# Graph attention on one core: node products and ACT's copies moved to the head of a step, products with Wv of the last units moved behind the last row products, sums and adds of the last units on POOL

## The chip, the cores and the metric

The kernel runs on one core of a Trainium2 chip. The metric is the device time of one execution in microseconds (us). The kernel before takes 2296.72 us, the median of 5 runs (2286.04 to 2301.53).

## What is computed

There are N = 12500 nodes with 128 features, and E = 212500 edges, sorted by their destination. An edge has 128 features and a weight. There are 8 heads of 16 features. Cut to what matters:

```
h = max(layernorm(x), 0)
q, v = h @ Wq.T + bq, h @ Wv.T + bv
k = edge_attr @ Wk.T + bk
in_m, out_m, diag_m = q[src].k, q[dst].k, q[src].q[dst]   # per edge and head
score = (softmax over dst of each of the three, summed) * weight ** lam
h = segment_sum(score * v[dst], dst)
out = x + leaky_relu(h @ Wo.T + bo, 0.1)
```

Since `v[dst]` is the same for all edges of a node, a node's h is v times a sum of scores. So the edges give each node three numerators and three denominators per head, and the nodes are finished from these sums.

## The kernel before

**Preparation.** The nodes are normalised and multiplied by Wq; q is written to a table in DRAM (`q_table`), and once more as three bf16 terms.

**The main loop over edges.** The edges are cut into 416 blocks of 512, and these into S = 5 streams, each of which runs through its own part of the edges. One pass of the loop, a *step*, takes a block of one stream: step number g is stream s = g % 5 of *turn* t = g // 5. There are 84 turns and 420 steps, and 10 more passes of the loop with no edges of their own. In a step:

- POOL issues four indirect DMAs (L656), each of which gathers 128 rows of q for a later block (`gather(g + 9)`), into one of 11 buffers `qq`.
- SP fetches edge features for block g + 6.
- PE makes k of block g + 1 (`project`, L1115 and L1117), spreads the q of the destinations by one-hot matrices (`spread_q`, L1126, "row products" below; ACT copies them to `qq`, L1128), and transposes the features of block g + 2 (`turn`, L1107; ACT copies them, L1109).
- DVE multiplies and reduces block g (`logits`, L1137, L1138, L1140). L1137 reads the gathered rows and the row products.
- ACT makes one-hots of block g + 3 (L1101, L1102).
- Once in a turn, for all five streams at a time and a turn or two later, come the softmax sums. At s = 0 PE transposes the logits (`l_ps`, L1153, `far_ps`, L1162) and the sums of the turn before (`b_ps`, L1226). At s = 1 DVE scans for the maximum (L1170, L1173). At s = 2 ACT makes the powers (`up`, `down`, `keep`, L1183 to L1188) and PE the sums by row (`w_ps`, L1239, copied by ACT, L1244). At s = 3 DVE multiplies (L1194) and makes two scans (L1198). At s = 4 PE shows where nodes end (`d_ps`, L1214), ACT makes `sel` of it (L1217, L1218), and SP writes the sums by row to DRAM (L1251).

**The nodes.** A *unit* is 256 nodes. Two units make an object of the class `Nodes`. Twenty pairs are finished within the loop, each over four turns from an even turn t on, when its sums are complete; they begin in turns 18, 22, 26, 30, 32 and so on, the last in turn 82:

- turn t: load sums and x (s = 0); normalise (ACT, s = 2 and 3); scores (six short DVE instructions on 96 or 32 columns, L1034 to L1039, s = 2)
- turn t + 1: transpose h (`turn`, L1043, copied by ACT, L1046, s = 1); the product with Wv (`project_v`: L1049 and L1051 on PE) and its weighing by the scores (DVE, L1059), s = 4
- turn t + 2: transpose (s = 1); the product with Wo (`project_o`: L1049 and L1051 on PE), 0.1 times it (ACT, L1069), the maximum (DVE, L1070) and the sum with x (DVE, L1071), s = 4
- turn t + 3: store (SP, s = 0)

All this stands in `nodes_between`, which is called near the end of a step. So PE's product at s = 4 comes behind the step's row products, transposes and d_ps, and DVE's part comes behind the step's L1140.

**The last units.** Nine units, in five objects `rest` (the last has one unit), have sums that are complete only at the end, and for some of them in two parts. `begin_rest` loads and normalises their x, transposes it and makes the products with Wv in the last steps. Its argument `at` is g - 411; LOOK is 9, so `at` = 9 is the first of the ten passes without edges. The products stay in PSUM buffers that the main loop no longer needs. After the loop the sums are loaded, the two parts added (DVE, L1032), the scores made and weighed, and the same transposes, products and adds follow, one object behind the other.

**What sets the order.** Every instruction goes through `pin`, which ties it behind the instruction pinned before it on its engine. So the order on each engine is the order in which the Python code runs, and an engine that waits holds up all that is pinned behind. Small results in PSUM (l_ps, far_ps, att_ps, keep, w_ps, d_ps, b_ps and all node_ps) share three buffers:

```python
        def small(shape, name):
            return ps.tile(shape, F32, name=name, tag="small", bufs=3)
```

The row products qd_ps have one buffer, so PE can make the next ones only when DVE's L1137 has read it.

Of the kernel before, what the change touches and what calls it, by code (L numbers as in the profile page):

```python
# [10 lines left out]
AF = mybir.ActivationFunctionType  # L11
# [9 lines left out]
SLOPE = 0.1  # L21
# [451 lines left out]
def ordered_path(ctx: ExitStack, tc: tile.TileContext, flag, x, src, dst, edge_attr, edge_weight,  # L473
# [19 lines left out]
    nc = tc.nc  # L493
    N, F = x.shape
    E = src.shape[0]
    P = 128
    NI = -(-N // P)
    NP = P * NI
    BE, JN = 512, 4
    NB = -(-E // BE)  # L500
    S = 5
    T = (NB + S - 1) // S
# [18 lines left out]
    def parts_of(u):  # L521

        return [s for s in range(S)
                if (s == 0 or START * s + RATE - NEAR < UN * (u + 1))
                and (s == S - 1 or UN * u < START * (s + 1) + RATE + NEAR)]

    def stored_at(u):

        of = parts_of(u)
        t = -(-(UN * (u + 1) + NEAR - START * of[0]) // RATE)  # L530
        return t + 2 if len(of) == 1 and t < T else None
# [57 lines left out]
    LOOK, QQ, AHEAD, EA = 9, 11, 6, 7  # L589
# [6 lines left out]
    def pin(inst):  # L596

        engine = str(inst.ins.engine)
        if engine in pinned:
            tc.add_manual_dep(inst.ins, pinned[engine], mybir.DependencyInfo(  # L600
                mybir.DependencyClass.NoSync, mybir.DependencyReason.DATA), reason="in order")
        pinned[engine] = inst.ins.name
        return inst
# [48 lines left out]
    def gather(g):  # L652
        if g < S * T:
            qq = gath.tile([P, JN, 2, F], F32, name="qq")
            for j in range(JN):
                rows = pin(nc.gpsimd.indirect_dma_start(  # L656
                    out=qq[:, j, 0, :], out_offset=None, in_=q_table,
                    in_offset=bass.IndirectOffsetOnAxis(
                        ap=src_i[:, g % S * G + g // S, j:j + 1], axis=0)))
                if (g - LOOK, j) in behind:  # L660
                    tc.add_manual_dep(rows.ins, behind[g - LOOK, j], mybir.DependencyInfo(
                        mybir.DependencyClass.Sync, mybir.DependencyReason.SCHED_ONLY),
                        reason="close behind the products")
            qqs[g] = qq
# [15 lines left out]
    with tc.tile_pool(name="prep", bufs=1) as prep, \  # L680
# [22 lines left out]
        for s in range(S):  # L703
            at = s * G * BE
            pin(nc.sync.dma_start(bases[:, :, s:s + 1], dst[None, at:at + G * BE + 1:BE, None]))
            n = min(T, (E - at) // BE)
# [287 lines left out]
    class Nodes:  # L994
# [26 lines left out]
        def normalize(self, lo, hi):  # L1021
            if lo == 0 and self.h is None:
                self.h = fin.tile([P, JN, F], F32, name="h", bufs=4)
            for b in range(lo, min(hi, self.n)):
                n = 2 * self.of[b // 2] + b % 2
                pin(nc.scalar.activation(self.h[:, b, :], self.x[:, b, :], AF.Relu,
                                         bias=shift[:, n:n + 1], scale=inv[:, n:n + 1]))

        def scores(self):
            n = self.n  # L1030
            for ab, more in self.more:
                pin(nc.vector.tensor_add(ab, ab, more))  # L1032
            den, num = self.ab[:, :n, 0:H3], self.ab[:, :n, H3:]
            pin(nc.vector.tensor_scalar(den, den, 1e-30, None, op0=ALU.max))  # L1034
            pin(nc.vector.reciprocal(den, den))
            pin(nc.vector.tensor_mul(num, num, den))
            score = self.score = fin.tile([P, JN, HEADS], F32, name="score")
            pin(nc.vector.tensor_add(score[:, :n], num[:, :, 0:HEADS], num[:, :, HEADS:2 * HEADS]))
            pin(nc.vector.tensor_add(score[:, :n], score[:, :n], num[:, :, 2 * HEADS:]))  # L1039
# [12 lines left out]
                                     stop=(b == self.n - 1)))  # L1052

        def project_v(self, to):
            self.product(to, bv3, wv)
            self.weigh(to)

        def weigh(self, to):
            pin(nc.vector.tensor_mul(  # L1059
# [5 lines left out]
        def project_o(self, to):  # L1065
            n = self.n
            self.product(to, bo3, wo)
            o, y = self.h[:, :n], self.x[:, :n]
            pin(nc.scalar.activation(o, to[:, :n], AF.Copy, scale=SLOPE))  # L1069
            pin(nc.vector.tensor_max(o, o, to[:, :n]))  # L1070
            pin(nc.vector.tensor_add(y, o, y))  # L1071

        def store(self):
            for i, u in enumerate(self.of):
# [8 lines left out]
    pairs, todo = {}, sorted((stored_at(u), u) for u in range(NU) if stored_at(u) is not None)  # L1083
# [3 lines left out]
    rest = [u for _, u in todo] + [u for u in range(NU) if stored_at(u) is None]  # L1087
    rest = [Nodes(rest[i:i + 2]) for i in range(0, len(rest), 2)]

    with tc.tile_pool(name="work", bufs=2) as work, \  # L1090
# [56 lines left out]
        def small(shape, name):  # L1147
            return ps.tile(shape, F32, name=name, tag="small", bufs=3)
# [106 lines left out]
        def later(f, t):  # L1255
            if 0 <= t < T:
                f(t)

        def nodes_between(t, s):
            new, old = pairs.get(t - t % 2), pairs.get(t - t % 2 - 2)  # L1260
            even = t % 2 == 0
            if new and even and s == 0:
                new.load_sums()
                new.load_x()
            if new and even and s == 2:
                new.normalize(0, 2)
                new.scores()
            if new and even and s == 3:
                new.normalize(2, 4)
            if new and not even and s == 1:  # L1270
                new.turn(small([P, JN, P], "node_ps"))
            if new and not even and s == 4:
                new.project_v(small([P, JN, F], "node_ps"))
            if old and even and s == 1:
                old.turn(small([P, JN, P], "node_ps"))
            if old and even and s == 4:
                old.project_o(small([P, JN, F], "node_ps"))
            if old and not even and s == 0:
                old.store()

# [6 lines left out]
        def spare():  # L1287
            return gath.tile([P, JN, 2, F], F32, name="qq").rearrange("p j i f -> p (j i f)")

        def halves():  # L1290
            return spare().rearrange("p (i j f) -> i p j f", i=2, j=JN)

        def begin_rest(at):
            if at in turned:
                late.update(zip(turned[at], halves()))
            if at in (LOOK - 1, LOOK):
                late[at - LOOK] = spare()
            for r, (of, begin) in enumerate(zip(rest, starts)):
                if at == begin:
                    to, of.h = halves()  # L1300
                    of.load_x(to)
                if at == begin + 2:
                    of.normalize(0, 4)
                if at == begin + 3:
                    of.hT = late[r]
                    of.turn(small([P, JN, P], "node_ps"))
                if at == LOOK + r:
                    of.held = ps.tile([P, JN, F], F32, name=holds[r], bufs=2 if r < 4 else 1)
                    of.product(of.held, bv3, wv)

# [10 lines left out]
        one_hots(2)  # L1321
        for g in range(end + 2 * S):
            s, t = g % S, g // S
            if g < end:
                gather(g + LOOK)
                fetch_edges(g + AHEAD)
            if g + 1 < end:
                project(g + 1)
                behind[g + 1, 0] = pinned[products]
                spread_q(g + 1)  # L1330
            if g + 2 < end:
                turn(g + 2)
            if g < end:
                logits(g)
            one_hots(g + 3)
            if s == 0:
                later(turn_logits, t - 1)
                later(turn_sums, t - 2)
            elif s == 1:
                later(scan_max, t - 1)  # L1340
            elif s == 2:
                later(powers, t - 1)
                later(to_rows, t - 2)
            elif s == 3:
                later(select, t - 1)
                later(scan_sums, t - 1)
                fetch(t + 2)
                fetch_rows(t + 2)
            else:
                later(show_ends, t - 1)  # L1350
                later(put_rows, t - 2)
            behind[g + 1, 2] = pinned[products]
            nodes_between(t, s)
            begin_rest(g - (end - LOOK))
            if g < S:
                of = [u for u in range(NU) if g in parts_of(u)]
                pin(nc.scalar.dma_start(
                    units(sums[g], of[0], len(of), 2 * H3),
                    blank[:, None, :].to_broadcast([P, len(of), 2 * 2 * H3])))


        for r, of in enumerate(rest):
            of.load_sums(*[late[k][:, r * JN * 2 * H3:(r + 1) * JN * 2 * H3].rearrange(
                "p (j c) -> p j c", j=JN) for k in (-1, 0)])
        for r in range(len(rest) + 2):
            if r < len(rest):
                rest[r].scores()
                rest[r].weigh(rest[r].held)
            if 0 <= r - 1 < len(rest):
                rest[r - 1].turn(small([P, JN, P], "node_ps"))  # L1370
            if 0 <= r - 2:
                rest[r - 2].project_o(small([P, JN, F], "node_ps"))
                rest[r - 2].store()


# [43 lines left out]
```

## Time and profile before

| what | us |
|---|---|
| median of 5 runs (lowest, highest) | 2296.72 (2286.04, 2301.53) |
| the profiled execution's own time | 2303.96 |
| its span, first to last instruction | 2302.2 |
| first L1137 on DVE, at | 144.15 |
| last L1137 on DVE, at | 2242.94 |
| first and last gather issued by POOL, at | 96.23, 2217.01 |
| granted TensorE clock, mean | 0.805 |

| engine | busy us | share |
|---|---|---|
| DVE | 2072.5 | 90% |
| PE | 1823.9 | 79% |
| ACT | 1650.1 | 72% |
| POOL | 1646.8 | 72% |

The lines of the profile that are quoted below have one of three forms. A group of instructions reads: line, engine, operation, out<-in, shapes, how often | busy us in all, mean ns of one | idle time before them, and what ended it. A wait reads: who <- whom: us in all, times, the longest. A line of the timeline reads: start, us, engine, line, operation, out<-in, how often, and in brackets the idle time of the engine before it and what ended that. "issue" stands for idle time in which the engine waited for nothing that the profile shows.

### The profile page before, as it was taken

Reading aid. Unit: us, or ns where it says so; the run is one execution under the profiler, and the core shown is the slowest. Engines: PE = TensorE matmul, PEld = TensorE weight load, DVE = VectorE, ACT = ScalarE, POOL = GpSimd, SP = SyncE. Lnnn points to the kernel's source line nnn. Section 1 sums busy time; section 2 is a strip of 40 time slices with the busy share of each in tenths; the row PEclk is TensorE's granted clock in tenths of the full one; section 3 lists DMA queues with packets and bytes.
Section 4 is the critical chain, followed back from the end, with each engine's and each line's share of the span. In section 5 each row is a group of like instructions: output and inputs, shape, how many; then the busy total and the mean of one; then the engine's idle time right before and its main releaser. Section 6 shows DMA issues by size and latency. Waiting matters only on the chain.

```text
span 2302.2 us, 36583 instructions
## 1 busy us (share of the span) xinstructions
PE 1823.9 (79%) x10781; PEld 1399.6 (61%) x10781; DVE 2072.5 (90%) x2180; ACT 1650.1 (72%) x3049; POOL 1646.8 (72%) x1716
## 2 busy tenths in 40 slices
PE   5538787878888888888888887888888878888885
PEld 4426565656666666666666666656666666666664
DVE  6779999989999999889999999998989899988984
ACT  5667777767777777677776777777777677776772
POOL 3577777777777777777777777777777777777740
PEclk8768889877877887779787788777777788877877
DMA  7785555555455555455554555555555555554531
GB/s 194 224 270 156 157 140 155 142 148 142 136 147 142 151 146 161 135 144 144 158 144 138 150 154 145 141 155 137 142 145 149 149 145 143 159 145 134 154 78 41
DMA packets 308902, 341.93 MB, mean 149 GB/s; under 512 B 139781, under 2 KB 227610, under 8 KB 308383
## 3 DMA queue, kind: packets, MB, share of 16 engines
q1 hardware_dynamic: 246259, 223.55, 32.6%
q0 software_dynamic: 54448, 112.96, 19.7%
q10 hardware_dynamic: 7984, 3.00, 0.5%
q8 instruction: 86, 1.41, 0.3%
q14 instruction: 125, 1.02, 0.1%
HBM read 308.22 MB, written 31.07 MB: 147 GB/s over the span
## 4 chain that ended last, share of the span: by engine, by line
PE 33%; ACT 22%; DVE 16%; DMA 13%; issue 12%; POOL 3%; SPq 1%; DVEq 0%; ACTq 0%; POOLq 0%
PE k_ps L1117 11%; DMA qq<-q_table,src_i 9%; PE eT_ps L1107 5%; ACT eT L1109 4%; PE qd_ps L1126 4%; DVE prod L1137 4%; ACT relb L1101 4%; DVE sum L1198 4%; ACT oh L1102 4%; DVE prod L1138 3%; ACT l L1160 3%; ACT qq L1128 3%; PE b_ps L1226 3%; POOL qq L656 3%; PE k_ps L1115 2%
## 5 line engine op out<-in xcount | busy, mean ns | idle before, releaser
L656 POOL DMA_INDIRECT qq<-q_table,src_i x1680 | 1609.9, 958 | 523.0 <-issue 318.5
L1140 DVE TENSOR_REDUCE lT<-prod 128x96 f32<-128x1536 f32 x420 | 736.3, 1753 | 14.3
L1117 PE MATMUL k_ps<-wk,eT 128*128 128x128 f32 x3360 | 603.4, 334 | 107.7 <-ACT eT L1109 65.8
L1117 PEld LDWEIGHTS k_ps<-wk,eT 128*128 128x128 f32 x3360 | 510.0, 232 | 253.3 <-ACT eT L1109 149.6
L1128 ACT COPY qq<-qd_ps 128x512 f32<-128x512 f32 x420 | 244.6, 582 | 456.3 <-PE qd_ps L1126 384.5
L1138 DVE TENSOR_TENSOR prod<-qq,k_ps 128x1024 f32<-128x1024 f32 x420 | 510.0, 1214 | 0.0
L1126 PE MATMUL qd_ps<-win,oh 126*128 126x128 bf16 x1680 | 199.6, 253 | 182.3 <-DVE prod L1137 166.3
L1137 DVE TENSOR_TENSOR prod<-qq,qd_ps 128x512 f32<-128x512 f32 x420 | 284.3, 677 | 65.4 <-ACT qq L1128 49.2
L1107 PE MATMUL eT_ps<-ident,ea 128*128 128x128 f32 x1680 | 326.2, 329 | 5.6 <-DVE found L955 5.6
L1101 ACT ACTIVATE relb<-relb,before 126x512 bf16<-126x512 bf16 x420 | 306.6, 730 | 0.0
L1126 PEld LDWEIGHTS <-oh 126*128 126x128 bf16 x1680 | 156.7, 115 | 217.2 <-issue 185.1
L1102 ACT ACTIVATE oh<-relb 126x512 bf16<-126x512 bf16 x420 | 264.6, 630 | 17.6 <-DMA qq<-q_table,src_i 4.3
L1109 ACT COPY eT<-eT_ps 128x512 f32<-128x512 f32 x420 | 247.3, 589 | 38.3 <-PE eT_ps L1107 36.3
L1107 PEld LDWEIGHTS eT_ps<-ident,ea 128*128 128x128 f32 x1680 | 230.9, 174 | 5.9 <-DVE found L955 5.9
L1226 PE MATMUL b_ps<-ident,sum 120*128 120x120 f32 x672 | 136.6, 333 | 112.8 <-ACT l L1160 112.8
L1226 PEld LDWEIGHTS b_ps<-ident,sum 120*128 120x128 f32 x672 | 99.1, 213 | 153.4 <-ACT l L1160 130.2
L1239 PE MATMUL w_ps<-back,sel 128*126 128x144 f32 x1344 | 190.9, 296 | 0.6 <-ACT back L1227 0.6
L1115 PE MATMUL k_ps<-b,ones 3*128 3x512 bf16 x420 | 185.7, 442 | 3.8 <-DVE prod L1138 3.4
L1239 PEld LDWEIGHTS w_ps<-back,sel 128*126 128x126 f32 x1344 | 172.7, 191 | 22.9 <-issue 18.7
L1227 ACT COPY back<-b_ps 128x480 f32<-128x480 f32 x168 | 97.5, 581 | 44.1 <-PE b_ps L1226 44.1
L1170 DVE TENSOR_TENSOR_SCAN u<-l,u,far_ps 120x512 f32<-120x512 f32 x83 | 105.5, 1271 | 1.8 <-ACT l L1160 1.8
L1198 DVE TENSOR_TENSOR_SCAN sum<-keep,sum,up 120x512 f32<-120x512 f32 x83 | 106.0, 1277 | 0.0
(187 smaller groups left out, 1857.8 us busy)
## 6 DMA issues: line engine op xcount, KB each, us to landing
ea<-in_edge_attr_dram SPq DMA_DIRECT2D x419, 256.0 KB
relb<-rel_d SPq DMA_DIRECT2D x84, 630.0 KB
qq<-q_table,src_i POOLq DMA_INDIRECT x1680
win<-q_table SPq DMA_DIRECT2D x420, 31.5 KB
q_table<-q SPq DMA_DIRECT2D x24, 384.0 KB
fa<-fa_d SPq DMA_DIRECT2D x420, 4.0 KB
sums<-rows SPq DMA_DIRECT2D x416, 7.9 KB
q_table<-xq SPq DMA_DIRECT2D x24, 256.0 KB
```

Source lines behind the costliest of these rows:

```text
L656: rows = pin(nc.gpsimd.indirect_dma_start(out=qq[:, j, 0, :], out_offset=None, in_=q_table, in_offset=bass.IndirectOffsetOnAxis(ap=src_i[: ...
L1101: pin(nc.scalar.activation(d, d, AF.Abs, bias=before[:K3]))
L1102: pin(nc.scalar.activation(oh, d, AF.Relu, bias=1.0, scale=-1.0))
L1107: pin(nc.tensor.transpose(eT_ps[:, j, :], eas[g][:, j * F:(j + 1) * F], ident))
L1109: pin(nc.scalar.copy(eT, eT_ps))
L1117: pin(nc.tensor.matmul(k_ps[:, j, :], eTs[g][:, j, :], wk, start=False, stop=(j == JN - 1)))
L1126: pin(nc.tensor.matmul(qd_ps[:, j, :], ohs[g][:, j * P:(j + 1) * P], d["win"][:, s, :], start=(j == 0), stop=(j == JN - 1)))
L1128: pin(nc.scalar.copy(qqs[g][:, :, 1, :], qd_ps))
L1137: pin(nc.vector.tensor_mul(prod[:, :, 2, :], qqs[g][:, :, 0, :], qds[g]))
L1138: pin(nc.vector.tensor_mul(prod[:, :, 0:2, :], qqs[g], ks[g][:, :, None, :].to_broadcast([P, JN, 2, F])))
L1140: pin(nc.vector.tensor_reduce(lTs[t][:, :, s, :], prod.rearrange("p j i (h d) -> p j (i h) d", d=DIM), AX.X, ALU.add))
L1239: pin(nc.tensor.matmul(w_ps[:, i].rearrange("p s c -> p (s c)"), d["sel"][:, j, lo:lo + 3, :].rearrange("p s w -> p (s w)"), d["back"][:, ...
```

## The change

1. A new function `nodes_before` is called at the head of each step. It makes the products of a pair at s = 4 (with Wv in odd turns, with Wo in even ones) and, with Wo, ACT's copy. They stood at the end of the same step. DVE's part (`weigh`; `add_x`, the maximum and the sum with x) stays at the end of the step.
2. The second transpose of the pair that ends after the loop's last turn (t = 84) is made at s = 2 in place of s = 1.
3. For the last units, the products with Wv move from `at` = 9, 10, 11, 12, 13 to `at` = 12, 13, 16, 16, 16, and the transpose of the fifth object from `at` = 9 to 12. In the steps 425 to 429 the last b_ps comes at `at` = 14 and the last w_ps at `at` = 16, ahead of the products there.
4. For the last units, POOL makes the sums of the two parts (`add_sums`, all objects one after the other, ahead of the first scores) and the sum with x. For the pairs in the loop there are no two parts to add, and DVE makes the sum with x as before.

```diff
+        def add_sums(self):
+            for ab, more in self.more:
+                pin(nc.gpsimd.tensor_add(ab, ab, more))
+
         def scores(self):
             n = self.n
-            for ab, more in self.more:
-                pin(nc.vector.tensor_add(ab, ab, more))
...
         def project_v(self, to):
+            self.held = to
             self.product(to, bv3, wv)
-            self.weigh(to)
...
         def project_o(self, to):
             n = self.n
             self.product(to, bo3, wo)
+            o = self.h[:, :n]
+            self.held = to
+            pin(nc.scalar.activation(o, to[:, :n], AF.Copy, scale=SLOPE))
+
+        def add_x(self, engine):
+            n, to = self.n, self.held
             o, y = self.h[:, :n], self.x[:, :n]
-            pin(nc.scalar.activation(o, to[:, :n], AF.Copy, scale=SLOPE))
             pin(nc.vector.tensor_max(o, o, to[:, :n]))
-            pin(nc.vector.tensor_add(y, o, y))
+            pin(engine.tensor_add(y, o, y))
...
+        def nodes_before(t, s):
+
+            new, old = pairs.get(t - t % 2), pairs.get(t - t % 2 - 2)
+            if new and t % 2 == 1 and s == 4:
+                new.project_v(small([P, JN, F], "node_ps"))
+            if old and t % 2 == 0 and s == 4:
+                old.project_o(small([P, JN, F], "node_ps"))
...
             if new and even and s == 2:
                 new.normalize(0, 2)
+                new.add_sums()
                 new.scores()
...
             if new and not even and s == 4:
-                new.project_v(small([P, JN, F], "node_ps"))
-            if old and even and s == 1:
+                new.weigh(new.held)
+            if old and even and s == (1 if t < T else 2):
                 old.turn(small([P, JN, P], "node_ps"))
             if old and even and s == 4:
-                old.project_o(small([P, JN, F], "node_ps"))
+                old.add_x(nc.vector)
...
-                if at == begin + 3:
+                if at == (begin + 3 if r < 4 else LOOK + 3):
                     of.hT = late[r]
                     of.turn(small([P, JN, P], "node_ps"))
-                if at == LOOK + r:
+                if at == LOOK + (3, 4, 7, 7, 7)[r]:
...
             s, t = g % S, g // S
+            nodes_before(t, s)
...
+        for of in rest:
+            of.add_sums()
         for r in range(len(rest) + 2):
...
                 rest[r - 2].project_o(small([P, JN, F], "node_ps"))
+                rest[r - 2].add_x(nc.gpsimd)
                 rest[r - 2].store()
```

## The prediction

> **What bounds the kernel now.** I read the busy shares first, then the waits, then the timeline turn by turn. On the page DVE looks like the bound, and the table of waits shows the idle time this change is aimed at:
>
> ```profile
> PE 1823.9 (79%) x10781; PEld 1399.6 (61%) x10781; DVE 2072.5 (90%) x2180; ACT 1650.1 (72%) x3049; POOL 1646.8 (72%) x1716
> ...
> L656 POOL DMA_INDIRECT qq<-q_table,src_i x1680 | 1609.9, 958 | 523.0 <-issue 318.5
> ```
>
> ```profile
> DVE h L1070 <- ACT h L1069: 52.3, 20, 4.1
> ...
> DVE h L1059 <- PE node_ps L1051: 28.5, 19, 1.9
> ```
>
> DVE stands still 80.8 us in 39 places, 76.6 us of it in 38 places of turns 18 to 82 of the main loop (the DVE waits of 200 to 2240 us: 48.1 + 28.5). One place, in the timeline of PE and DVE:
>
> ```profile
> 2057.74 0.59 PE L1126 MATMUL qd_ps<-win,oh 126*128 126x128 bf16 x4 [2.89 <-DVE prod L1137]
> ...
> 2059.78 0.63 PE L1049 MATMUL node_ps<-b,ones 3*128 3x512 bf16 x1
> 2060.34 2.08 PE L1051 MATMUL node_ps<-wo,hT 128*128 128x128 f32 x8
> ...
> 2063.35 0.69 DVE L1070 TENSOR_TENSOR h<-h,node_ps 128x512 f32<-128x512 f32 x1 [2.74 <-ACT h L1069]
> ```
>
> PE idles 2.89 us just before step 4's row products, makes the node product after them, and DVE then waits for it.
>
> But look at POOL. Its row reads 72%, yet there are 1680 gathers of 0.94 us with 0.30 us between them, whatever releaser is named: one starts each 1.25 us, without a break, from 96 to 2217 us. Twenty gathers are a turn: 25.0 us, with a few long ones 25.16. How far is DVE behind them? I compare the last gather of a step with the product (L1137) that reads it, at step 0 of turn 14 (first two rows) and of turn 83 (last two), in the timeline; the row between is step 3 of turn 15:
>
> ```profile
> 461.39 0.94 POOL L656 DMA_INDIRECT qq<-q_table,src_i  x1 [0.30 <-issue]
> 465.57 0.68 DVE L1137 TENSOR_TENSOR prod<-qq,qd_ps 128x512 f32<-128x512 f32 x1
> ...
> 480.37 0.69 DVE L1137 TENSOR_TENSOR prod<-qq,qd_ps 128x512 f32<-128x512 f32 x1 [1.55 <-DMA qq<-q_table,src_i]
> ...
> 2196.71 0.94 POOL L656 DMA_INDIRECT qq<-q_table,src_i  x1 [0.30 <-issue]
> 2221.23 0.68 DVE L1137 TENSOR_TENSOR prod<-qq,qd_ps 128x512 f32<-128x512 f32 x1
> ```
>
> The lead of the gathers (end of issue to use) is 37 us at the start and is eaten by turns without nodes, which take DVE 22.43 us at least. It is 3.2 us in turn 14 (465.57 - 462.33), and in the row between DVE waits for a gather. From turn 18 on the nodes cost DVE more: from 566.1 to 2221.2 us it takes 25.46 us a turn, and the gathers, from 562.3 to 2197.7, 25.16. So the lead grows again, from 3.8 us (turn 18) to 23.6 us (turn 83). **Both engines are within 0.30 us a turn of being the bound**; DVE can win back what it has fallen behind, and no more.
>
> **The change, part by part.**
>
> Products and ACT's copies at the head of step 4. Nothing is added: the same 9 matmuls (0.37 + 1.16 us at the full clock, 0.63 + 2.08 at the half), one ACT copy of 0.58 us, the same DVE instructions in the same order. PE now has the product before step 4's k and row products, where it idled 0.9 to 3.5 us (38 places). At the full clock (1.5 us) the idle time hides it; at the half clock (2.6 us) it makes the row products up to 1.7 us late. Behind them on PE's queue stand the key transposes and d_ps; who waits is DVE's next L1137, which comes after L1138 (1.21), L1140 (1.75) and 0.69 or 1.38 us of node work, 3.6 us or more after the current one, while row product and ACT copy need 0.63 + 0.59. That leaves 2.4 us of cover, so I cost the move at nothing; without the cover it is 1.7 us in each of 38 turns. ACT's copy stands before the row copy instead of behind the one-hots; no ACT instruction ahead of k's needs is behind it. No DMA or queue is passed by in the loop except the store, whose source is ready earlier.
>
> So DVE's demand falls by 76.6/65 = 1.18 us to 24.28 us a turn, below POOL's 25.16. What is late next is the gather: DVE catches up and waits for POOL, as in turns 14 to 19, where the lead at step 0 was 3.2, 3.0, 4.7, 4.8, 3.8, 4.1 us. I take 4.5 us in turn 83, bounded by 3.0 and by 8.0 (the largest in turns 18 to 31). Gain: 23.6 - 4.5 = **19.1 us** (15.6 to 20.6). The other 57 us of removed waits come back as waits for gathers; by the same account the lead falls to its least already when a quarter of the waits go (25.46 - 0.30 = 25.16).
>
> The tail, part one: products with Wv behind the last row products. After DVE's last L1140 (end 2246.5) PE is the queue to watch:
>
> ```profile
> 2246.66 1.08 PE L1153 MATMUL l_ps<-ident,lT 128*120 128x128 f32 x4 [1.95 <-DVE lT L1140]
> ...
> 2250.62 2.08 PE L1051 MATMUL eT_ps<-wv,qq 128*128 128x128 f32 x8
> ...
> 2255.98 0.69 DVE L1194 TENSOR_TENSOR ew<-up,att_ps 120x512 f32<-120x512 f32 x1 [5.09 <-ACT up L1187]
> ...
> 2264.70 2.23 PE L1239 MATMUL w_ps<-back,sel 128*126 128x144 f32 x16 [0.65 <-ACT back L1227]
> ...
> 2272.79 0.26 DVE L1032 TENSOR_TENSOR qq<-qq 128x96 f32<-128x96 f32 x1 [8.20 <-DMA qq<-sums]
> ...
> 2282.84 0.69 DVE L1070 TENSOR_TENSOR qq<-qq,node_ps 128x512 f32<-128x512 f32 x1 [1.78 <-ACT qq L1069]
> ...
> 2294.95 0.43 DVE L1071 TENSOR_TENSOR qq<-qq 128x256 f32<-128x256 f32 x1
> ```
>
> ACT's `up` waits today behind a node copy that waits for the first late product; with turn and product behind it, the scans end about 3.4 us sooner (`up` would start at gap's end, 2250.9, not 2254.28). PE loses three products from the queue before the last b_ps: 1.40 + 1.41 + 0.65 = 3.46 us (the starts 2257.61, 2259.01, 2260.42 and 2262.18 to 2262.83). The last w_ps then starts some 2.9 us sooner: ACT's sel and node copies take back 0.6. Bounds 0 (ACT's queue binds) and 3.9 (all of the scan's and PE's relief). The moved products stand in the 5.9 us between w_ps's end and the arrival of the sums (2266.9 to 2272.8): hidden.
>
> Part two: six DVE sums (0.25 us) and five DVE adds (four of 0.69, one of 0.43) go to POOL, which has nothing to issue then. No POOL add is in the trace. Its casts (L769, 104x2050 in 1.88 us, 0.92 ns an element) and its tensor_scalar (L773, 104x2048 in 7.12 us, 3.47 ns) bound a 512-element add by 0.47 and 1.78 us; with two inputs I take 1.0 us, nearest to two passes of the cast, and 0.5 us for a sum of 96 elements. The first scores then start 0.2 us later than now. From there, in order: DVE's scores and weighing 2.4 us a unit; the third unit's at +7.2; the first L1070 at +9.3, held by transpose, product, copy at the half clock (4.5 us from the second weighing, as now); the fourth's scores to +12.4; L1070s at +16.65, +18.5, +19.2; POOL's last two adds to +20.8. Now it is 22.3 us (2273.09 to 2295.38). Gain 1.5 - 0.2 = **1.3 us** (0.3 to 2.1).
>
> One page speaks against this edit. The Trainium skill, "GPSIMD Engine Reference", section "Elementwise — side-by-side cycle accounting", has a two-input add of 2048 elements at 4497 ns on GPSIMD and 2293 on VectorE, a ratio of 1.96, and advises VectorE. By it the add is an estimated 1.36 us instead of DVE's 0.69, and the gain 0.9 us instead of 1.3; no row of this trace has such an add.
>
> **Sum.** 19.1 + 2.9 + 1.3 = 23.3 us. The profiled execution took 2303.96 us (span 2302.2): 2280.7 us. It lies 7.2 us above the median of the runs, 2296.72. The gathers' floor is the same in every run, so I read the runs' spread (2286.04 to 2301.53) as different lags, and keep 2280.7; if the whole execution were merely longer, the same sum off the median gives 2273.4.
>
> **Rivals.**
>
> 1. *DVE is the only bound*: all 76.6 us and the tail count, 2303.96 - 76.6 - 4.2 = 2223. For it: DVE 90% busy, largest share. Against it: the gathers' unbroken 1.25 us, and turns 14 to 19. 3%.
>
> 2. *The waits come back*: the product finds its PSUM buffer (one of three shared ones) taken and starts late, or PE at the half clock is late for the next L1137. It takes nine tenths of the 76.6 us to keep most of the lag: DVE's demand is then 25.34, the lead in turn 83 about 3.8 + 65 x 0.18 = 15.5, the gain 8 + 4: 2292; with all of them and no gain in the tail 2304. For it: PE's half clock in most of these places. Against it: the idle time and the 2.4 us of cover. 9%.
>
> 3. *Slower*: the product must wait for the buffer that the decay scans (L1198) hold until step 4's L1137 starts. At the half clock product 2.63, k 2.61, row products 0.63 and copy 0.59 end 6.5 us later, against DVE's 4.3 or 5.0: waits of 2.2 and 1.5 us, and 1.6 us more at the next step, where PE (1.06 + 0.88 + 2.63 + 0.63) is still behind. 19 x 3.8 + 19 x 3.1 = 131 us in place of 76.6: 2304 + 54 - 4 = 2354. It decides from 2.4 us a place: 0.4 above today's mean of 2.0 (76.6 over 38) is the 15.5 us that cancel the tail's 4 and add 0.5%. Against it: a late unit's transposes write such a buffer at 2227.1 before the scan at 2228.3 has read far_ps, the oldest of the three; buffers are not dealt in strict turn. 9%.
>
> **Numbers.** The POOL floor has 79%: 2280.7, its own range 2270 to 2287 (lead 3 to 8 us, tail 0.3 to 6, and the median's offset). To hold 8 in 10 the range takes in part of rival 2: 2268 to 2292. About 0.5% (11.5 us, to 2285.2) is what a measurement of this kernel can tell from no change. Faster by more: 93 of 100 in the floor case, and rival 1: 0.76. Within: the rest of the floor case and rival 2, 0.15. Slower: 0.09.
>
> **What will show it.** The waits L1070 on L1069 and L1059 on the node product gone from the loop; in their place DVE or ACT waiting for gathers; the lead at step 0 of turn 83 near 4.5 us; gathers still each 1.25 us, the last near 2217; PE's idle time before step 4's row products shorter; L1194's 5.09 us gone; POOL adds of about 1 us. I am wrong if gathers slow down, if L1137 at step 0 waits for ACT's row copy, or if the lead still grows.

## The result: no change

The changed kernel takes 2295.11 us, the median of 26 runs (2288.78 to 2299.59), the kernel before 2295.9 (47 runs, 2286.04 to 2303.84): a ratio of 0.9995 (95% interval 0.9988 to 1.0003). Predicted were 2280.7. In some of the experiments below (groups A to C) the median of the kernel before was 2887 to 2902 us instead of 2296; every ratio is against the kernel before in the same group. Single runs more than 1.5% above the fastest of the same kernel are left out of the times and ratios.

**Up to turn 82 the loop did what was predicted.** The profiled execution of the changed kernel took 2293.29 us (span 2291.4). Lines have moved: L1137 is now L1144, L1140 L1147, L1059 L1061, L1069 to L1071 are L1072, L1077 and L1078, L1043 L1045, L1117 L1124, L1126 L1133, L1128 L1135, L1194 L1201, L1239 L1246. The waits of DVE for node products are gone from its list for 200 to 2240 us, which now begins (total, times, longest):

```profile
DVE prod L1144 <- DMA qq<-q_table,src_i: 69.9, 48, 3.8
DVE prod L1144 <- ACT qq L1135: 33.2, 49, 2.7
```

So DVE now waits for gathers. Gathers still start each 1.25 us, and at step 0 of turn 83 their lead is 2200.94 - 2195.90 = 5.0 us, in place of 23.6; predicted were 4.5:

```profile
2194.96 0.94 POOL L656 DMA_INDIRECT qq<-q_table,src_i  x1 [0.30 <-issue]
...
2200.94 0.68 DVE L1144 TENSOR_TENSOR prod<-qq,qd_ps 128x512 f32<-128x512 f32 x1
```

**The end did not.** After POOL's last add there stands POOL's own end. The sequencers' rows by line (count, shortest/median/longest in ns, first to last start), in the changed kernel first the row ahead of the drain and then the drains:

```profile
L1408 POOLq INC_SWDGE_SEM  x1: 2155/2155/2155, 2280.3 to 2280.3; - x1
```

```profile
L1434 POOLq DRAIN  x3: 46/103/8076, 2282.5 to 2291.1; - x3
L1434 SPq DRAIN  x3: 7/7/13, 2284.1 to 2290.8; - x3
```

and the drains in the kernel before:

```profile
L1414 POOLq DRAIN  x3: 46/103/8076, 2228.9 to 2301.9; - x3
L1414 SPq DRAIN  x3: 7/7/13, 2301.3 to 2301.6; - x3
```

The first of POOL's drains takes 8.08 us, behind an INC_SWDGE_SEM of 2.16 us and some 3 us of waits and branches. This end follows POOL's last instruction, whatever that is. Before, that was a short zero fill (L990, over at 2223.5) behind the last gather: the drain was over at 2237.0, 64 us before SP's last store had ended (SP's first drain, 2301.3). Now POOL's last add ends at 2277.24, its drain at 2282.48 + 8.08 = 2290.56, and SP is done at 2284.1. **POOL ends last, 6.5 us after SP.**

The span, piece by piece, against the profiled execution that the prediction used, and against a second profile of the kernel before (last experiment), an execution of 2294.18 us:

| piece | predicted | first profile of before to the changed | second profile of before to the changed |
|---|---|---|---|
| start of the last L1137/L1144 | -19.1 | 2242.94 to 2225.89: -17.1 | 2231.27 to 2225.89: -5.4 |
| end of the last reduce to the last w_ps | -2.9 | 18.2 to 16.2: -2.0 | 19.1 to 16.2: -2.9 |
| last w_ps to the end of the last add | -1.3 | 30.7 to 31.6: +0.9 | 31.6 to 31.6: 0.0 |
| end of the last add to the span's end | 0 | 6.8 to 14.2: +7.4 | 6.8 to 14.2: +7.4 |
| span | -23.3 | 2302.2 to 2291.4: -10.8 | 2292.4 to 2291.4: -1.0 |

Of the 7.4 us, 6.5 are POOL's drain after SP is done; the rest is SP, which is done 6.9 us after the last add in place of 5.9.

### The profile page after: what moved, and what is told of

The parts are those of the page before. It is cut to its first block, busy times and chain, and to the rows that moved or that the text cites. A ratio compares the mean times of both kernels' runs of the same rounds, so it can differ in the third digit from the quotient of the medians.

```text
span 2291.4 us, 36554 instructions
## 1 busy us (share of the span) xinstructions
PE 1794.8 (78%) x10781; PEld 1377.0 (60%) x10781; DVE 2069.1 (90%) x2169; ACT 1651.2 (72%) x3049; POOL 1652.6 (72%) x1727
## 4 chain that ended last, share of the span: by engine, by line
PE 27%; DVE 19%; ACT 19%; DMA 17%; issue 13%; POOL 3%; SPq 1%; DVEq 0%; ACTq 0%; POOLq 0%
DMA qq<-q_table,src_i 13%; PE k_ps L1124 10%; DVE prod L1144 5%; PE eT_ps L1114 4%; PE qd_ps L1133 4%; DVE prod L1145 4%; DVE sum L1205 4%; ACT relb L1108 3%; ACT eT L1116 3%; ACT oh L1109 3%; POOL qq L656 3%; ACT qq L1135 3%; ACT l L1167 3%; PE b_ps L1233 2%; PE k_ps L1122 2%
## 5 line engine op out<-in xcount | busy, mean ns | idle before, releaser
L1147 DVE TENSOR_REDUCE lT<-prod 128x96 f32<-128x1536 f32 x420 | 736.3, 1753 | 14.3
L1124 PE MATMUL k_ps<-wk,eT 128*128 128x128 f32 x3360 | 598.0, 332 | 82.2 <-ACT eT L1116 41.4
L1124 PEld LDWEIGHTS k_ps<-wk,eT 128*128 128x128 f32 x3360 | 504.8, 230 | 232.6 <-ACT eT L1116 134.4
L1135 ACT COPY qq<-qd_ps 128x512 f32<-128x512 f32 x420 | 244.7, 583 | 435.9 <-PE qd_ps L1133 368.9
L1144 DVE TENSOR_TENSOR prod<-qq,qd_ps 128x512 f32<-128x512 f32 x420 | 284.8, 678 | 125.9 <-DMA qq<-q_table,src_i 78.2
L1133 PE MATMUL qd_ps<-win,oh 126*128 126x128 bf16 x1680 | 196.9, 251 | 231.0 <-DVE prod L1144 214.2
L1114 PE MATMUL eT_ps<-ident,ea 128*128 128x128 f32 x1680 | 321.0, 325 | 5.6 <-DVE found L955 5.6
L1133 PEld LDWEIGHTS <-oh 126*128 126x128 bf16 x1680 | 156.9, 114 | 271.7 <-issue 263.3
L1233 PE MATMUL b_ps<-ident,sum 120*128 120x120 f32 x672 | 141.8, 344 | 98.9 <-ACT l L1167 98.9
L1246 PE MATMUL w_ps<-back,sel 128*126 128x144 f32 x1344 | 197.3, 302 | 0.7 <-ACT back L1234 0.6
L1246 PEld LDWEIGHTS w_ps<-back,sel 128*126 128x126 f32 x1344 | 178.6, 197 | 23.2 <-issue 16.4
```

Of the source, the lines that this page charges most:

```text
L1114: pin(nc.tensor.transpose(eT_ps[:, j, :], eas[g][:, j * F:(j + 1) * F], ident))
L1124: pin(nc.tensor.matmul(k_ps[:, j, :], eTs[g][:, j, :], wk, start=False, stop=(j == JN - 1)))
L1133: pin(nc.tensor.matmul(qd_ps[:, j, :], ohs[g][:, j * P:(j + 1) * P], d["win"][:, s, :], start=(j == 0), stop=(j == JN - 1)))
L1135: pin(nc.scalar.copy(qqs[g][:, :, 1, :], qd_ps))
L1144: pin(nc.vector.tensor_mul(prod[:, :, 2, :], qqs[g][:, :, 0, :], qds[g]))
L1147: pin(nc.vector.tensor_reduce(lTs[t][:, :, s, :], prod.rearrange("p j i (h d) -> p j (i h) d", d=DIM), AX.X, ALU.add))
```

## The experiments

Theory A: the loop's gain is real but small in an ordinary execution, and POOL's exposed end takes it back. Theory B: the earlier products save next to nothing. Theory C: what costs is only the length of POOL's adds.

### The changed kernel with sums and adds back on DVE

```
-                pin(nc.gpsimd.tensor_add(ab, ab, more))
+                pin(nc.vector.tensor_add(ab, ab, more))
...
-        for of in rest:
-            of.add_sums()
...
+                rest[r].add_sums()
                 rest[r].scores()
...
-                rest[r - 2].add_x(nc.gpsimd)
+                rest[r - 2].add_x(nc.vector)
```

Group A:

> The changed kernel with the sums and the last adds of the tail on DVE again; all else as changed. Theory A (the loop's gain is real, some 7 us at the median, and is given back because POOL's own end, 14 us from its last instruction, is now the last thing to finish): the stretch from the last compute to the end of the span falls from 14.15 us to about 7, POOL's drain lies some 60 us before the end, and the time is 2288 to 2289 us, 6 to 7 below the changed kernel. Theory B (the profiled execution of before was only longer as a whole; the earlier products save next to nothing in an ordinary execution): 2293 to 2295 us. Theory C (what costs is the slower adds themselves, 1.26 us each, and DVE slowed beside them): 1 to 2 us below the changed kernel, 2293 to 2294, with the end after the last compute still near 14 us.

Group B:

> The changed kernel with the sums and the last adds of the tail on DVE again, once more, because the first time the kernel before took 2902 us (not 2296) and gathers were no floor. Where the kernel before takes about 2296 us: theory A (the loop's gain at the median is some 7 us and is given back because POOL's own end, 14 us from its last instruction, is the last thing to finish) 2288 to 2289, the last compute to the span's end about 7 us; theory B (in an ordinary execution the earlier products save next to nothing) 2293 to 2295; theory C (only the slower adds cost) 2293 to 2294 with 14 us at the end. Where before takes about 2900 again: 3.4% faster, as in the first call.

Last group, where the kernel before took 2293.55 us:

> The changed kernel with all gathers, the sums and the last adds of the tail on DVE, a third time; in the call before this one the kernel before took 2293 us again. Where it does so: theory A 2286 to 2289, 6 to 7 below the changed kernel (the price of POOL's end, 10 us at most by the last call), the last compute to the span's end about 7 us, and the loop ends at the gathers' floor: lead 4 to 6 us at step 0 of turn 83. Theory C: 2293 to 2294.

Measured: 0.9657 (0.9632 to 0.9682) in A, 0.9626 (0.9592 to 0.9660) in B, and in the last group **0.9972 (0.9959 to 0.9984), 2285.6 us**. Its drain is hidden again, and the last add ends at 2275.74, 6.8 us before the end:

```profile
L1433 POOLq DRAIN  x3: 46/103/8076, 2220.8 to 2282.2; - x3
L1433 SPq DRAIN  x3: 7/7/13, 2281.6 to 2281.9; - x3
```

Against the change's 0.9995 this is 0.0023, or 5.3 us (2 to 9 with both intervals): what POOL's part costs. From the last w_ps to the last add it takes 31.6 us with the adds on either engine, so the adds' length is not the price, and theory C falls. This kernel beats both others; in its profile the lead at step 0 of turn 83 is 7.1 us, a little above the 4 to 6 expected.

### Parts alone, and where POOL's end lies

Products only (groups A and B):

```
 before.py
+            nodes_before(t, s)
...
+                new.weigh(new.held)
...
+                old.add_x(nc.vector)
```

> Before with only the products and ACT's copies of the loop put at the head of step 4; the tail as before. Theory A: the loop's gain alone, 5 to 8 us, 2288 to 2291 us; the gathers' lead over DVE at step 0 of turn 83 is 3 to 6 us as in the changed kernel. Theory B: within 2 us of before, 2294 to 2297 us. By the recorded prediction it would be 19 us, 2277.

> Before with only the products and ACT's copies of the loop moved, once more. Where before takes about 2296 us: theory A 2288 to 2291, lead of the gathers at step 0 of turn 83 3 to 6 us; theory B 2294 to 2297. Where before takes about 2900: 3.1% faster, as in the first call.

Measured: 0.9687 (0.9664 to 0.9710) and 0.9655 (0.9623 to 0.9687). Beside them the kernel before took 2902 and 2888 us: they tell nothing of the floor, since the gathers were no floor there (their lead at step 0 was 45 to 54 us in every turn, in the changed kernel of group C too).

POOL's part only (groups A and B):

```
 before.py
+                pin(nc.gpsimd.tensor_add(ab, ab, more))
+                rest[r - 2].add_x(nc.gpsimd)
```

> Before with only the six sums and the last adds of the tail put on POOL. Theory A: POOL's last instruction stands 1 to 2 us after the last DVE instruction, its end of 14 us follows, the stretch from the last compute to the end of the span is about 14 us in place of 6.8; 6 to 8 us slower than before, 2302 to 2304 us. Theory C: 1 to 2 us slower. By the recorded prediction 1.3 us faster.

> Before with only the sums and the last adds of the tail on POOL, once more. In the first call it was 5.8 us slower (ratio 1.0022, 1.0003 to 1.0041), the size that theory A gives for POOL's exposed end. Theory A: 6 to 8 us slower, 2302 to 2304 where before takes 2296. Theory C: 1 to 2 us slower.

Measured: 1.0022 (1.0003 to 1.0041) and 1.0025 (0.9999 to 1.0050): 6 and 7 us slower, as theory A has it. In the second of these, POOL's drain ends at 2881.7 + 8.1 = 2889.8, SP is done at 2883.9.

Late products only, with part 2 of the change (group A):

```
 before.py
-            if old and even and s == 1:
+            if old and even and s == (1 if t < T else 2):
...
-                if at == begin + 3:
+                if at == (begin + 3 if r < 4 else LOOK + 3):
...
-                if at == LOOK + r:
+                if at == LOOK + (3, 4, 7, 7, 7)[r]:
```

> Before with only the tail's products with Wv (and the turns ahead of them) put behind the last row products. All theories: last w_ps 2 to 3 us sooner after the last product of DVE, 2293 to 2294 us; the prediction had 2.9. If the late products are not hidden where they stand now, no gain: 2296.

Measured: 0.9979 (0.9965 to 0.9994), 6 us faster, with 2 to 10 in the interval. The direction holds; the size agrees no better than that.

One copy by POOL at the very end (group B), which takes no add from DVE:

```
 before.py
+        pin(nc.gpsimd.tensor_copy(rest[-1].score[:, 0, 0:1], rest[-1].x[:, 0, 0:1]))
```

> Before with one copy of a single element a partition by POOL, which waits for the last add of DVE (it writes a buffer that nothing reads); everything else as before. Theory A: POOL's end sequence starts only then; from the copy to POOL's last instruction about 14 us against SP's end some 7 us after the add, so 6 to 8 us slower than before. Theory C: no add is on POOL, so no cost: within 1 us of before.

Measured: 1.0038 (1.0010 to 1.0067), 3 to 19 us slower for one instruction that nothing waits for; 6 to 8 were expected. POOL ends last, 7.5 us after SP (2875.1 + 8.1 against 2875.7):

```profile
L1415 POOLq DRAIN  x3: 46/103/8076, 2875.1 to 2883.7; - x3
L1415 SPq DRAIN  x3: 7/7/13, 2875.7 to 2883.4; - x3
```

This shows the cause: POOL's place at the end costs even when POOL takes over no work. The changed kernel itself, and with the adds alone back on DVE (group C):

> The changed kernel itself, once more, beside the kernel before on the same chip. In the two calls so far the kernel before took 2887 to 2902 us, with the results of PE reaching ACT some us after their records end; there the moved products alone gave 3.1 and 3.5% and POOL's part alone cost 0.2%. If that comes again: theory D (there PE's late results are on the path and the earlier products take them off it) 3.0 to 3.4% faster, some 6 us slower than the same kernel with the adds on DVE. If before takes 2296 again: 2295, as measured.

```
 after.py
-                rest[r - 2].add_x(nc.gpsimd)
+                rest[r - 2].add_x(nc.vector)
```

> The changed kernel with the sums on POOL as changed, and only the adds with x at the end back on DVE: POOL's last instruction is then a sum, some 20 us before the last add, so that its end is hidden again. Theory A: 6 to 7 us below the changed kernel, 0 to 1 above the kernel with both on DVE; POOL's drain ends before SP's. Theory C (only the adds' own length costs): 1 to 2 us below the changed kernel.

Measured: 0.9649 (0.9615 to 0.9684) and 0.9631 (0.9593 to 0.9668), 2790.3 and 2782.6 us: the size of theory A, but the two intervals overlap. The places are clear: with the sums alone on POOL, its drain is over at 2749.7 + 8.1 = 2757.8 and the span ends at 2771.3.

### The floor, taken away

Half of the gathers left out, before (group C):

```
+            pin(nc.sync.dma_start(qq[:, 2:, 0, :], q_table[0:2 * P, :].rearrange("(j p) f -> p j f", p=P)))
-            for j in range(JN):
+            for j in range(2):
                 rows = pin(nc.gpsimd.indirect_dma_start(
```

> Before with half of the gathers left out (of each step's four, the last two are replaced by one plain load of fixed rows on SP's queue, so those rows are not the ones of the edges): POOL issues 10 gathers a turn, 12.5 us, and is no floor. Where before takes 2296: DVE's 25.46 us a turn was the bound in most turns, so 5 to 30 us faster, about 2270 to 2290. Where before takes about 2890: PE's late results bind, not the gathers, so less than 1% off.

The same with the products moved:

> The same with half of the gathers left out, and the loop's products and copies moved as in the change. Theory A with the gathers as floor, where before takes 2296: without the floor the removed waits are won, 60 to 80 us below the kernel with half of the gathers and the products unmoved. If gathers are not what gave the gain back: 10 us or less between the two. Where before takes about 2890: theory D expects the same 3 to 3.5% between the two as with all gathers.

Measured: 2288.92 and 2231.95 us, so **57 us** (2.5%) for the moved products where DVE waits for no gather, a little less than either expectation (60 to 80 us, or 3 to 3.5%). The expectation for the first, less than 1% off 2890, was wrong: without half of the gathers the whole 600 us by which this group was longer are gone (last section).

### The floor, put back (kernel before at 2293.22 us in this group)

```
                 if j < 2:
                     rows = pin(nc.gpsimd.indirect_dma_start(
...
+                else:
+                    rows = pin(nc.gpsimd.memset(fill, 0.0))      # fill: 1 x 1390, f32
```

> Before, with the last two gathers of each step left out (those rows come from one plain load of fixed rows on SP's queue, so they are not the edges' rows), and in the place of each left-out gather a write of zeros by POOL over 1390 elements of one partition, about 1.25 us by the rate of the zero fills of this trace (8x2048 in 1.80 us). POOL is so again busy 1.25 us for each of the four, 25 us a turn, but without the gathers beside which PE's results came late. All theories: near the kernel with half of the gathers and no filling, 2289 us; with the floor 0 to 10 more, 2289 to 2299.

> The same as the first of this call (half of the gathers left out, POOL filled with writes of zeros), with the loop's products and copies moved as in the change. Theory A (POOL's 25 us a turn is the floor that DVE runs into): of the 57 us that the move is worth without the filling, 5 to 20 are left, 2275 to 2290. Rival (the floor doesn't hold the gain back; the waits came back in another form): 50 to 60 us, 2235 to 2245, as without the filling.

> The whole change, with half of the gathers left out and POOL filled with writes of zeros in their place. Theory A: the loop's gain less POOL's exposed end: within 5 us of the first kernel of this call, as the change was of before; some 4 us above the second.

> The same as the third of this call (half of the gathers left out, POOL filled), with the sums and the last adds of the tail on DVE again. Theory A: POOL's end is hidden again, 6 to 8 us below the third, 1 to 3 below the second. Theory C (only the adds' own length costs): 1 to 2 us below the third.

| half of the gathers, POOL filled | us | against before (95%) | lead, step 0 of turn 83 |
|---|---|---|---|
| before | 2289.00 | 0.9973 (0.9948 to 0.9998) | 39.8 |
| products moved | 2253.34 | 0.9827 (0.9804 to 0.9849) | 5.6 |
| whole change | 2256.57 | 0.9845 (0.9823 to 0.9866) | 5.9 |
| whole change, POOL's part on DVE | 2246.43 | 0.9805 (0.9784 to 0.9827) | 5.9 |

The lead in the first of these four kernels, and then in the second:

```profile
2155.36 0.94 POOL L660 DMA_INDIRECT qq<-q_table,src_i  x1 [0.30 <-issue]
...
2196.09 0.68 DVE L1143 TENSOR_TENSOR prod<-qq,qd_ps 128x512 f32<-128x512 f32 x1
```

```profile
2157.31 0.94 POOL L660 DMA_INDIRECT qq<-q_table,src_i  x1 [0.30 <-issue]
2158.25 2.55 POOL L665 MEMSET fill<- 1x1390 f32 x2
...
2163.88 0.68 DVE L1150 TENSOR_TENSOR prod<-qq,qd_ps 128x512 f32<-128x512 f32 x1
```

POOL is as far in both at that point; DVE has come up to it in the second. The gain is 34 us by the two ratios (26 to 41 with their intervals), neither the 5 to 20 of theory A nor the rival's 50 to 60. The filling was too short: a turn of POOL takes 24.7 us here (mean of turns 18 to 80), not the 25.16 of the real gathers, and 0.4 us over 65 turns is an estimated 26 us of floor that was not there. So the whole change, expected within 5 us of the first kernel, lies some 30 us below it. The lead does fall to 3 to 6 us, from about turn 46 on, and stays there: the floor ends the gain, at the height that POOL's turn sets. Theory B falls. The last two rows differ by 10.1 us, 2 to 16 by the ratios, where 6 to 8 were expected: POOL's end again. The last lies 5 us by the ratios below the second, where 1 to 3 were expected.

### How much lead there was to win

> The kernel before itself, for a second profiled execution. If the first one (2303.96 us, DVE 25.46 us a turn from turn 18 to 83, lead 23.6 us at the end) was an unusually long one, as the change's 19 us of predicted and 0.8 us of measured gain suggest: here DVE's turn is 25.2 to 25.3 us and the lead at step 0 of turn 83 is 10 to 16 us, in an execution of 2290 to 2297 us. If the lead is 20 us or more also here, the loop's gain was 15 us or more and the tail must have lost it all.

Measured: 0.9993 (0.9980 to 1.0007), as it must be. The profiled execution took 2294.18 us:

```profile
2196.54 0.94 POOL L656 DMA_INDIRECT qq<-q_table,src_i  x1 [0.30 <-issue]
...
2212.25 0.68 DVE L1137 TENSOR_TENSOR prod<-qq,qd_ps 128x512 f32<-128x512 f32 x1
```

The lead is 2212.25 - 2197.48 = 14.8 us, and DVE takes 25.32 us a turn (turns 18 to 83), not 25.46. DVE's waits for node products from 200 to 2240 us are 59.7 us here, not 76.6: those for the product with Wv, 28.5 us in 19 places there, are 11.4 us in 7. So the profile that the prediction was made from, at 2303.96 us, lies above all 47 runs of that kernel (of the later runs of this condition one was longer, 2305.91) and had 9 us of lag more than this ordinary one. Two profiles do not show how the lag is spread over executions.

## Why the prediction was wrong, step by step

Three terms of the sum failed: POOL's end, which it did not have (7.4 us in the profile); the 19.1 us, which one long execution had to give and an ordinary one has not; and the cost of the move, put at nothing, which turn 83 pays (about 3 us beside the first profile, 6 beside the second).

- *"Gain: 23.6 - 4.5 = 19.1 us"*. Right for the execution it was read from (the lead fell to 5.0; the last product of DVE starts 17.1 us sooner), and the mechanism, that DVE runs into POOL's pace, is shown by the pairs of kernels without and with moved products, once without a floor and once with one. As the gain of the kernel it was mis-sized: an ordinary execution has 14.8 us of lead, not 23.6, so 9.8 us to win at that point.
- *"That leaves 2.4 us of cover, so I cost the move at nothing"*. Up to turn 82 this holds: from 560 us on, DVE's products wait for ACT 33 us in the changed kernel, against 31 and 33 in the two profiles of before (40 in the kernel with the adds on DVE; with half of the gathers left out, 39 before the move and 33 after). In turn 83, where the transposes of the late units stand on PE's queue, it does not. DVE waits there, in the changed kernel, 5.6 us:

```profile
2205.09 0.69 DVE L1144 TENSOR_TENSOR prod<-qq,qd_ps 128x512 f32<-128x512 f32 x1 [0.55 <-ACT qq L1135]
...
2213.32 0.69 DVE L1144 TENSOR_TENSOR prod<-qq,qd_ps 128x512 f32<-128x512 f32 x1 [2.65 <-ACT qq L1135]
...
2217.57 0.69 DVE L1144 TENSOR_TENSOR prod<-qq,qd_ps 128x512 f32<-128x512 f32 x1 [0.65 <-ACT qq L1135]
...
2225.89 0.69 DVE L1144 TENSOR_TENSOR prod<-qq,qd_ps 128x512 f32<-128x512 f32 x1 [1.75 <-ACT qq L1135]
```

  The first profile of before has 2.6 us there, the second none. It is not that the lag had covered these waits. In the kernel with half of the gathers left out and the products moved, the gathers are 50 us ahead of the last product, and DVE waits 4.8 us all the same:

```profile
2147.55 0.69 DVE L1146 TENSOR_TENSOR prod<-qq,qd_ps 128x512 f32<-128x512 f32 x1 [0.55 <-ACT qq L1137]
...
2154.23 0.69 DVE L1146 TENSOR_TENSOR prod<-qq,qd_ps 128x512 f32<-128x512 f32 x1 [1.15 <-ACT qq L1137]
...
2158.49 0.69 DVE L1146 TENSOR_TENSOR prod<-qq,qd_ps 128x512 f32<-128x512 f32 x1 [0.65 <-ACT qq L1137]
...
2167.45 0.69 DVE L1146 TENSOR_TENSOR prod<-qq,qd_ps 128x512 f32<-128x512 f32 x1 [2.40 <-ACT qq L1137]
```

  Over all profiles, the twelve of kernels with moved products have 3.2 to 7.0 us of waits in turn 83, the eight without them 0 to 2.7 us, whatever the lead. PE, which makes what that copy waits for, in the changed kernel:

```profile
2200.36 1.11 PE L1045 MATMUL node_ps<-ident,qq 128*128 128x128 f32 x4 [2.23 <-DVE h L1077]
...
2210.18 2.08 PE L1124 MATMUL k_ps<-wk,eT 128*128 128x128 f32 x8
2212.04 0.62 PE L1133 MATMUL qd_ps<-win,oh 126*128 126x128 bf16 x4
...
2221.83 0.66 PE L1045 MATMUL node_ps<-ident,qq 128*128 128x128 f32 x4 [3.67 <-DVE ew L1201]
```

  By the releasers that the trace names, a late unit's transposes wait for a PSUM buffer twice: for the one of the node product, which is written earlier now and held until DVE's maximum L1077, and for one that DVE's multiplication L1201 still reads. In the second profile of before the same transposes (L1043, at 2209.78 and 2227.67) do not wait the first time, and 2.30 us the second. k and the row products stand behind them. A second part is PE's clock: k takes 2.0 to 2.1 us in three of these four steps, in that profile of before in one, and 1.16 us in the others. What of the waits is due to which, and why the clock differs, is not shown. By the last product, 3.8 us of the 9.8 are left (lead 13.8 and 10.0 us), and 1.6 us more come from gathers that end sooner.
- *"The last w_ps starts some 2.9 us sooner"*: 2.0 and 2.9 us. Right.
- *"Six DVE sums and five DVE adds go to POOL, which has nothing to issue then. Gain 1.3"*. Two faults. The small one: from the last w_ps on nothing is won. An add of 512 elements takes 1.26 us, not 1.0 (a sum of 96 takes 0.39, not 0.5); two of DVE's multiplications are slower beside it; and the time that DVE saves turns into waits for ACT's copies L1072, 6.4 us ahead of the maxima against 4.3 with the adds on DVE. This answers the disputed price: by the ratio of 1.96 in the Trainium skill, "GPSIMD Engine Reference", section "Elementwise — side-by-side cycle accounting", the prediction had an estimated 1.36 us; here it is 1.26 against 0.69 us, 1.83. The rows:

```profile
2264.57 1.26 POOL L1078 TENSOR_TENSOR qq<-qq 128x512 f32<-128x512 f32 x1 [7.60 <-DVE qq L1077]
2265.43 0.52 DVE L1038 TENSOR_TENSOR qq<-qq 128x96 f32<-128x96 f32 x1
...
2267.80 1.26 POOL L1078 TENSOR_TENSOR qq<-qq 128x512 f32<-128x512 f32 x1 [1.97 <-DVE qq L1077]
2268.34 0.79 DVE L1038 TENSOR_TENSOR qq<-qq 128x48 f32<-128x48 f32 x1
```

  The multiplications in the second and fourth row take 0.26 and 0.21 us with the adds on DVE. The large fault: "nothing to issue" was read as free. What POOL still has to do, its end sequence of some 13 us (2277.24 to 2290.56), was in the trace of before and hidden (2223.5 to 2237.0); work that is given to POOL later moves it. It costs 7.4 us of the profile, and 5.3 us by the runs with and without POOL's part.
- *"I keep 2280.7"*. The argument, that the floor makes the changed kernel's time independent of the lag of the one profiled, holds: the changed kernel's last product starts at 2225.9, predicted was 2242.9 - 19.1 = 2223.8. Of the 12.6 us between 2280.7 and the profiled 2293.29, 7.4 are POOL's end, 2.2 the adds (0.9 of them also lie between the two profiles of before), 2.1 the loop and 0.9 the w_ps. Without POOL's part 2285.6 us were measured, within the range. But the same argument meant that the kernel's gain is to be taken from its ordinary lag, not from the one execution that lay 7 us higher, and the chances for "no change" were made without that.
- Rivals 1 to 3: DVE as the only bound fell (2223 was far off) but would have been near where gathers are no floor (57 us); the waits that clearly come back do so in turn 83 alone; the held PSUM buffers cost PE 2.2 and 3.7 us there, not in each turn, and so nothing like the 131 us of rival 3.

## What to carry to other kernels

Before giving late work to an idle engine, look at what that engine does after its last instruction: here POOL's end takes 13 us, while SP is done 6 to 7 us after the last add, so an add that POOL makes there lengthens the kernel. Where two engines are within a few tenths of a turn of each other, the gain of a faster one is the lag it has, in an ordinary execution and at the point where the loop ends; profile the kernel twice before a gain is read from one trace. And a move that costs nothing in most turns can cost in the last ones, where other work stands on the same queue and shares the same buffers: price it there by itself.

## What the runs showed that was not expected

In groups A to C the median of the kernel before was 2887 to 2902 us at a mean granted clock of 0.70 to 0.72, against 2293 to 2297 us and 0.79 to 0.81 in the others. There, PE's results reached ACT long after the ends of PE's rows. One place in the kernel with the one POOL copy:

```profile
1508.61 0.58 PE L1126 MATMUL qd_ps<-win,oh 126*128 126x128 bf16 x4 [0.85 <-issue]
...
1508.99 1.06 PE L1107 MATMUL eT_ps<-ident,ea 128*128 128x128 f32 x4
...
1511.79 0.59 ACT L1128 COPY qq<-qd_ps 128x512 f32<-128x512 f32 x1 [3.19 <-PE d_ps L1214]
...
1515.36 0.59 ACT L1109 COPY eT<-eT_ps 128x512 f32<-128x512 f32 x1 [2.98 <-remote]
```

ACT copies qd_ps 2.6 us after its matmuls' rows end (1509.19) and eT_ps 5.3 us after (1510.05), although it stood idle; in the changed kernel in the other condition it copies qd_ps 0.04 us after (2204.43 and 2204.47). The Trainium skill, "Perfetto Trace Analysis", section "Tensor Engine Instruction (MATMUL, LD_WEIGHTS)", says that a matmul's end in the trace is an estimate, so the rows do not show whether the matmul or its signal was late. Gathers ran 45 to 60 us ahead there from turn 1 on, no floor was in reach, and the same change gave 3.5% (ratio 0.9649). With half of the gathers left out, on the same chip and beside it, the lateness was gone (2289 us). That it goes away when half of the gathers are left out is shown; but that kernel also has POOL idle more and a plain load more on SP's queue, so which of these matters, and what sets the condition, stays open.
